# A two-way selective scan: one of four sums moved to TensorE and ScalarE, and decays kept from the forward to the backward pass

## The chip, the cores and the metric

The kernel runs on one core of one Trainium2 chip. The core has five engines that run beside each other, each through its own instructions in order: TensorE (PE in the profile; PEld are its weight loads), VectorE (DVE), ScalarE (ACT), GpSimd (POOL) and SyncE (SP), which here issues the DMA transfers. SBUF is the large on-chip memory, PSUM the small one that TensorE writes. The metric is the device time of one execution in microseconds; lower is better.

## What is computed

Four images of 64 x 64 pixels with 96 channels go through four layers: a selective-scan block, a convolution, attention with a feed-forward network, and a Fourier filter with a feed-forward network. The change concerns the scan of the first layer. Cut to what matters, the reference is:

```python
x_hwwh = jnp.stack([x_hw, x_wh], axis=0)                       # by rows, by columns
xs = jnp.concatenate([x_hwwh, jnp.flip(x_hwwh, axis=3)], axis=0)   # and both backwards
...
def step(h, inp):
    u_t, dt_t, B_t, C_t = inp
    dA = jnp.exp(dt_t[..., None] * A)                          # the decay
    h = dA * h + (dt_t * u_t)[..., None] * B_t[:, None, :]
    y = jnp.sum(h * C_t[:, None, :], axis=-1)
    return (h, y)
_, ys = jax.lax.scan(step, h0, (uT, dT, BT, CT))
...
yy = y[0] + wh_y + inv_y[0] + invwh_y
```

An image has 192 inner channels with 16 states each and 4096 positions. The forward and the backward scan of one orientation have the same decays `dA`, the same `dt * u * B` and the same `C`, so their states `h` can be added before they are multiplied by `C` and summed over the states.

## The kernel before

**Phases.** A phase is one group of 8 channels (with 16 states: 128 partitions) of one image in one orientation. There are 4 images x 2 orientations x 24 groups = 192 phases (`phases`, N = 192), in a loop over `n` in which the order of every engine's instructions is written out by hand (`manual_schedule`). The 4096 positions are cut into 4 chunks of 1024 (`CH`), numbered q = 0 to 3.

A phase has eight steps. In the first four (a loop over q, with the forward scan at L1677) DVE scans the chunks forwards into `S`, one after the other, each starting from the last column of the one before. In the other four (a loop over k, where k = 0 works on chunk 3 and k = 3 on chunk 0; the scan is at L1722) it scans them backwards. A backward scan writes over its own decays; a copy of one column (`edge`, L1728) carries the state on; then DVE adds the result to the forward one (L1729: `S = S + pa`).

Around DVE's scans:

- `load_delta` and `load_du` (their DMAs are recorded at L1412) fetch delta (`dl`) and delta times u (`B`) by chunk, in the order of SP's queue. `dl` and `S` have five buffers each: `place_of` gives a phase's chunks the places 0 to 3, and the next one's the places 4 to 1, so that a chunk's place comes free for the next phase's chunk 4 - q, and place 0 or 4 for chunk 0 of the phase after that. `B` has eight, two sets.
- `decay` (L1450) on ScalarE makes exp(A x delta) from `dl` into a PSUM buffer `pa`, of which there are two of two banks each. Those of chunks 3 and 2 serve both directions (chunk 2's is made a second time at q = 3, the two at hand then being chunk 3's and this one); those of chunks 1 and 0 are made anew at k = 1 and k = 2, and that of the next phase's chunk 0 at k = 3. That makes seven decays per phase.
- `times_b` (L1440) on POOL multiplies `B` by the states' B, `times_c` (L1444) multiplies the sum `S` by C. Their order in a phase is: at q = 0 to 3 `times_c` of chunk 0 of the phase before, `times_b` of chunk 3, `times_b` of chunks 0 and 1 of the next phase; at k = 0 `times_b` of its chunk 2; at k = 1 to 3 `times_c` of chunks 3, 2 and 1.
- `reduce` (L1460) on TensorE sums over the 16 states, four matmuls for each half of a phase; `result` (L1468) on ScalarE copies that out of PSUM, and `store_result` (L1477) stores it.

**The other stages.** While the scans run, the steps before them for images 1 to 3 (`main_lane`, then `before_scans`: projection, 3 x 3 convolution, gates) and the layers after them for images 0 to 2 (`rest`) are dealt out between the scans by `pieces(step)`: after each of the eight steps a table `gains` gives each engine some credit (the five columns are TensorE, ScalarE, POOL, DVE and DMA issue), and a piece of another stage is placed when its engine's credit covers its cost. They have three PSUM banks; the scans have five (four for the two `pa`, one for `py`). What is left of `rest` when the scans end is put before the last image's own layers.

**The steps that the prediction names:**

```python
later = decay(n, q + 1) if q < 3 else decay(n, 2)          # forward, one chunk ahead
...
nc.vector.tensor_tensor_scan(
    pa[:, ::-1], pa[:, ::-1], Bs[n, q][:, ::-1],
    edge if k else 0.0, ALU.mult, ALU.add,
)
if k < 3:
    edge = big.tile([128, 1], F32, tag="edge", name="edge", bufs=2)
    nc.vector.tensor_copy(edge, pa[:, 0:1])
nc.vector.tensor_tensor(Ss[n, q], Ss[n, q], pa, ALU.add)
```

Of the kernel before, what the change touches and what calls it, by code (L numbers as in the profile page):

```python
# [73 lines left out]
def layers(ctx: ExitStack, tc: tile.TileContext, a: dict, out):  # L74
# [1268 lines left out]
    def main_lane(take):  # L1343

        region = Region(tc)
        wk = region.sbuf("pre")
        images = [before_scans(b, wk, take, prev=b - 1 if b > 1 else None) for b in range(1, NB)]
        yield [chain(*parts) for parts in zip(*images)], [region, weights]
        for b in range(NB - 1):
            yield from rest(b, take, 1)  # L1350
# [17 lines left out]
    def last_place(name, k):  # L1368

        if (name, k) not in last_tiles:  # L1370
            tags = {
                "w_in": [f"B{4 * (N % 2) + q}" for q in range(4)],
                "sz_in": [f"dl{place_of(N - 1, q)}" for q in (3, 2, 1, 0)],
                "xr": [f"rep0{q}" for q in range(4)],
                "y_in": [f"B{4 - 4 * (N % 2) + q}" for q in range(4)],
            }
            t = big.tile([128, CH], F32, tag=tags[name][k // 2], name=name)
            for j in range(2):
                last_tiles[name, k // 2 * 2 + j] = t[:C, j * BLK : (j + 1) * BLK]
        return last_tiles[name, k]  # L1380
# [19 lines left out]
    def place_of(n, q):  # L1400


        return (4, 3, 2, 1)[q] if n % 2 else q
# [41 lines left out]

    def decay(n, q):
        if n < N:
            pa = ps.tile([128, CH], F32, tag="pa", name="pa", bufs=2)
            g = phases[n][1]
            nc.scalar.activation(pa, dls[n, q], AF.Exp, scale=nega[:, g : g + 1])  # L1450
            return pa

    def reduce(n, half):

        if n < 0:
            return
        py = pys[n, half] = ps.tile([128, BLK], F32, tag="py", name="py")
        for j in range(4):
            q, k = 2 * half + j // 2, j % 2
            nc.tensor.matmul(  # L1460
                py[32 * j : 32 * j + 32, :], lhsT=red, rhs=Ss[n, q][:, k * BLK : (k + 1) * BLK],
                start=True, stop=True,
            )

    def result(n, half):
# [17 lines left out]
    class Lane:  # L1483
# [34 lines left out]
    gains = [  # L1518
        (2.6, 0.7, 0, 0.8, 1.8), (1.4, 1.2, 0, 0.8, 0.8),
        (2.6, 1.2, 0, 0.8, 0.8), (2.6, 1.2, 0, 0.8, 0.8),  # L1520
        (3.8, 2.8, 1.2, 1, 1.6), (3.8, 2.4, 1.2, 1, 1.4),
        (3.8, 2.4, 1.2, 1, 1.0), (2.6, 2.4, 1.2, 1, 1.6),
    ]
    cap = (4.4, 3.0, 3.2, 1.6, 4.0)

    def pieces(step):
# [3 lines left out]
        for free, bank in returned:  # L1530
            free.append(bank)
        returned.clear()
        for e in range(5):

            more = 1.25 if e in (2, 4) and clock[0] > 8 * (N - NG) else 1
            credit[e] = min(cap[e], credit[e] + gains[step][e] * more)
        for lane in list(lanes):
# [79 lines left out]
    def first_loads():  # L1617
# [8 lines left out]
        for q in range(NCH):  # L1626
            load_rep(0, 1, q)
        for q in range(3):
            load_du(1, q)
# [16 lines left out]
    with tc.manual_schedule():  # L1646
        ordered[0] = True
        pa = decay(0, 0)
        for n in range(N + 1):
# [3 lines left out]
            for q in range(NCH):  # L1653

                if q == 1:
                    load_du(n + 1, 3)
                if q > 1:
                    load_delta(n + 1, q - 2)
                if n % NG == 0 and 0 < n < N and q > 0:
                    load_rep(h, 1, 4 - q)  # L1660
                later = decay(n, q + 1) if q < 3 else decay(n, 2)
                if q == 0:
                    times_c(n - 1, 0)
                elif q == 1:
                    times_b(n, 3)
                else:
                    times_b(n + 1, q - 2)
                if q == 1:
                    reduce(n - 1, 0)
                if q == 2:  # L1670
                    store_result(n - 1, 1)
                if end:
# [4 lines left out]
                nc.vector.tensor_tensor_scan(  # L1677
                    s, pa, Bs[n, q], Ss[n, q - 1][:, CH - 1 : CH] if q else 0.0, ALU.mult, ALU.add
                )
                if q < 3:  # L1680
                    pa = later
                pieces(q)
# [17 lines left out]
            for k, q in enumerate(reversed(range(NCH))):  # L1700
# [6 lines left out]
                if k == 1:  # L1707
                    store_result(n - 1, 0)
                if k == 2:
                    load_delta(n + 1, 3)  # L1710
                if k > 0:
                    load_du(n + 2, k - 1)
                if n % NG == NG - 2:
                    load_rep(h + 1, 0, k)
                if k == 1:
                    pa, later = later, decay(n, 1)
                elif k == 2:
                    pa, later = later, decay(n, 0)
                elif k == 3:
                    pa, later = later, decay(n + 1, 0)  # L1720

                nc.vector.tensor_tensor_scan(  # L1722
                    pa[:, ::-1], pa[:, ::-1], Bs[n, q][:, ::-1],
                    edge if k else 0.0, ALU.mult, ALU.add,
                )
                if k < 3:
                    edge = big.tile([128, 1], F32, tag="edge", name="edge", bufs=2)
                    nc.vector.tensor_copy(edge, pa[:, 0:1])  # L1728
                nc.vector.tensor_tensor(Ss[n, q], Ss[n, q], pa, ALU.add)  # L1729
                if k == 3:  # L1730
                    reduce(n, 1)
                pieces(4 + k)
                if n == N - 1:
                    for i in (2 * k, 2 * k + 1):
                        last_loads(last_place, i)
            pa = later
            if n % NG == NG - 4 and h + 1 < len(halves):
# [120 lines left out]
```

## Time and profile before

| what | us |
|---|---|
| median of 3 runs (lowest to highest) | 5898.77 (5889.44 to 5907.25) |
| the profiled execution | 5897.32 |
| its span, first to last instruction | 5895.5 |
| first scan starts | 359.2 |
| last sum of the scans ends | 5487.4 |

The mean TensorE clock that was granted in the profiled execution is 0.73 of full speed. The page's second part shows how evenly the middle is filled (40 slices of 147 us, each digit a busy share in tenths):

```profile
PE   8978888889873675553566764656467655566787
...
DVE  2049898899899998999899999999998999989464
ACT  4557766776664356545555456454634554545333
POOL 1258888889898667767678778776866777766300
PEclk9978888889875765566657865676576655785788
DMA  3258878887698878788988868686986568896203
```

To read it: DVE is near nine tenths from slice 4 to slice 37, which are the scans. The last three slices are the last image's layers, where TensorE works most. The DMA row is the mean busy share of the 16 DMA engines.

A row of the costliest groups reads: line, engine and operation, output <- inputs, shape, count | busy us in all, mean ns of one | idle time of the engine just before them, and what ended it. A row of waits reads: who <- for whom: us in all, times, longest.

### The profile page before, as it was taken

The page shows a single profiled execution, that of the slowest core. Times are in us where ns is not written, and L with a number is a line of the kernel's source. Part 1 is how long each engine was busy: PE and PEld are TensorE (multiplying, and loading weights), DVE is VectorE, ACT ScalarE, POOL GpSimd, SP SyncE. Part 2 cuts the span into 40 slices and gives each one's busy share as a digit, 9 for nine tenths or more (in the row PEclk, how much of TensorE's full clock was granted, in tenths as well). Part 3 has the DMA queues.
Part 4 walks back from the last instruction along what each step waited for, and adds up shares of the span by engine and source line. Part 5 has one row for each costly group of instructions (what it writes and reads, how often), then busy time and mean ns, then how long its engine had stood idle before and what let it go on. Part 6 is the DMA issues. An engine that isn't in the chain of part 4 may idle for free. (4 is left out here: it accounts for less than half of the span.)

```text
span 5895.5 us, 64395 instructions
## 1 busy us (share of the span) xinstructions
PE 4072.8 (69%) x19490; PEld 1646.2 (28%) x19490; DVE 4947.4 (84%) x3590; ACT 3235.1 (55%) x4358; POOL 4104.8 (70%) x1982
## 2 busy tenths in 40 slices
PE   8978888889873675553566764656467655566787
PEld 3322222223220121142321211433122114332245
DVE  2049898899899998999899999999998999989464
ACT  4557766776664356545555456454634554545333
POOL 1258888889898667767678778776866777766300
PEclk9978888889875765566657865676576655785788
DMA  3258878887698878788988868686986568896203
GB/s 99 77 158 236 226 208 223 244 243 206 187 248 238 229 199 222 202 227 246 254 228 229 211 169 222 203 239 187 239 224 182 158 190 234 248 242 184 57 30 112
DMA packets 469416, 1173.08 MB, mean 199 GB/s; under 512 B 90496, under 2 KB 155628, under 8 KB 468972
## 3 DMA queue, kind: packets, MB, share of 16 engines
q1 hardware_dynamic: 469068, 1168.97, 71.7%
q8 instruction: 154, 2.52, 0.2%
q14 instruction: 194, 1.59, 0.1%
HBM read 1011.86 MB, written 156.76 MB: 198 GB/s over the span
## 5 line engine op out<-in xcount | busy, mean ns | idle before, releaser
L1444 POOL TENSOR_TENSOR S<-S,rep 128x1024 f32<-128x1024 f32 x768 | 1807.1, 2353 | 965.1 <-DVE S L1729 885.1
L1450 ACT ACTIVATE pa<-dl,nega 128x1024 f32<-128x1024 f32 x1344 | 1498.5, 1116 | 1539.1 <-DVE S L1729 1175.0
L1440 POOL TENSOR_TENSOR B<-B,rep 128x1024 f32<-128x1024 f32 x768 | 1790.8, 2359 | 90.5 <-DMA B<-du_s 45.3
L1677 DVE TENSOR_TENSOR_SCAN S<-pa,S,B 128x1024 f32<-128x1024 f32 x576 | 1352.1, 2347 | 257.3 <-ACT pa L1450 86.1
L1722 DVE TENSOR_TENSOR_SCAN pa<-pa,edge,B 128x1024 f32<-128x1024 f32 x576 | 1354.0, 2351 | 66.7 <-ACT pa L1450 66.6
L1460 PE MATMUL py<-S,red 128*32 128x512 f32 x3072 | 630.9, 886 | 858.9 <-POOL S L1444 785.1
L361 PE MATMUL p_conv<-xp,conv_w 96*96 96x504 f32 (+3 forms) x2304 | 1056.4, 613 | 13.6 <-ACT u L374 11.5
L1729 DVE TENSOR_TENSOR S<-S,pa 128x1024 f32<-128x1024 f32 x768 | 932.2, 1214 | 6.6
L1677 DVE TENSOR_TENSOR_SCAN S<-pa,B 128x1024 f32<-128x1024 f32 x192 | 438.0, 2281 | 176.7 <-DMA rep<-bc_s 173.1
L361 PEld LDWEIGHTS p_conv<-xp,conv_w 96*96 96x96 f32 x2304 | 386.1, 171 | 669.0 <-issue 615.5
L1722 DVE TENSOR_TENSOR_SCAN pa<-pa,B 128x1024 f32<-128x1024 f32 x192 | 440.8, 2296 | 5.3
L1460 PEld LDWEIGHTS py<-S,red 128*32 128x32 f32 x3072 | 76.0, 128 | 1228.0 <-POOL S L1444 1009.6
L154 ACT COPY side<-side 96x256 f32<-96x256 f32 (+1 forms) x448 | 281.3, 628 | 52.9 <-DMA duT_s<-side 25.9
L1055 POOL CAST h<-y 128x1536 fp8e5<-128x1536 f16 x64 | 95.5, 1493 | 294.7 <-ACT y L766 284.2
L877 PE MATMUL p_mean<-t,centre 96*96 96x512 f32 x256 | 199.5, 895 | 117.7 <-ACT sq L869 48.8
L527 PE MATMUL p_y<-side,ident 96*96 96x512 f32 x336 | 215.2, 792 | 29.9 <-DMA side<-y_s 15.6
L1468 ACT COPY ys<-py 128x512 f32<-128x512 f32 x384 | 221.2, 576 | 19.6 <-PE py L1460 17.3
L929 PE MATMUL p_rstd<-rs_y,pick 32*96 32x512 f32 x256 | 168.4, 985 | 71.0 <-DVE ln L920 23.6
L833 PE MATMUL p_l<-x,taps 96*96 96x504 f32 (+3 forms) x432 | 202.8, 623 | 9.6 <-DMA x<-x 9.6
L1120 PE MATMUL p_h<-w1s,ln 97*64 97x64 f32 x2304 | 177.9, 346 | 36.7 <-DVE hb L1104 18.6
L1046 PE MATMUL p_f<-q,w_L 96*128 96x512 fp8e5 x192 | 98.2, 548 | 149.7 <-ACT y L757 75.6
L1120 PEld LDWEIGHTS p_h<-w1s,ln 97*64 97x64 f32 x2304 | 171.6, 251 | 78.2 <-issue 31.4
(210 smaller groups left out, 5059.4 us busy)
## 6 DMA issues: line engine op xcount, KB each, us to landing
dl<-delta_s SPq DMA_DIRECT2D x768, 256.0 KB
B<-du_s SPq DMA_DIRECT2D x768, 256.0 KB
B<-duT_s SPq DMA_DIRECT2D x768, 256.0 KB
dl<-deltaT_s SPq DMA_DIRECT2D x768, 256.0 KB
z_s<-z SPq DMA_DIRECT2D x48, 512.0 KB
zl<-z_s SPq DMA_DIRECT2D x64, 384.0 KB
side<-y_s SPq DMA_DIRECT2D x120, 192.0 KB
rep<-bc_s SPq DMA_DIRECT2D x64, 256.0 KB
```

What stands on the lines that cost most here:

```text
L154: nc.scalar.copy(o.rearrange("p (w h) -> p w h", h=HW), t[:n, :].rearrange("p (h w) -> p w h", w=HW)[:, q * w : (q + 1) * w, :],)
L361: nc.tensor.matmul(pr[:, ra:rb, ca_:cb_], lhsT=conv_w[:, kc, ky * 3 + kx, oc * C : (oc + 1) * C], rhs=xp[:, kc, at + ra : at + rb, ca_ + d ...
L527: nc.tensor.matmul(p, lhsT=ident[:C, :C], rhs=x, start=(j == 0), stop=(j == 2))
L1120: nc.tensor.matmul(p[at : at + N1, j, :], lhsT=ln3[:, 8 * k + j, :], rhs=w1s[:, hs], start=True, stop=True,)
L1440: nc.gpsimd.tensor_tensor(Bs[n, q], Bs[n, q], reps[n // NG, 0, q], ALU.mult)
L1444: nc.gpsimd.tensor_tensor(Ss[n, q], Ss[n, q], reps[n // NG, 1, q], ALU.mult)
L1450: nc.scalar.activation(pa, dls[n, q], AF.Exp, scale=nega[:, g : g + 1])
L1460: nc.tensor.matmul(py[32 * j : 32 * j + 32, :], lhsT=red, rhs=Ss[n, q][:, k * BLK : (k + 1) * BLK], start=True, stop=True,)
L1468: nc.scalar.copy(ys, pys.pop((n, half)))
L1677: nc.vector.tensor_tensor_scan(s, pa, Bs[n, q], Ss[n, q - 1][:, CH - 1 : CH] if q else 0.0, ALU.mult, ALU.add)
L1722: nc.vector.tensor_tensor_scan(pa[:, ::-1], pa[:, ::-1], Bs[n, q][:, ::-1], edge if k else 0.0, ALU.mult, ALU.add,)
L1729: nc.vector.tensor_tensor(Ss[n, q], Ss[n, q], pa, ALU.add)
```

## The change

Four things are changed together.

1. **One sum of four, on other engines.** From the phase on in which the steps before the scans are done for all images (`done["pre"]`), the sum of k = 3 (chunk 0) is not made by DVE. Instead `add_up` at q = 0 of the next phase lets TensorE add `S` and the backward result, each by two matmuls of 512 columns with the identity matrix, in a PSUM buffer; `take_sum` at q = 1 copies that to `S` on ScalarE. By the order of instructions these are 138 of the 192 phases: 54 to 191.
2. **Decays are kept.** Five decays per phase instead of seven. The two PSUM buffers have names now: chunk 0 and chunk 2 use `pa0`, chunk 3 uses `pa1`; chunk 1's decay is written over `dl` in SBUF and stays there until its backward scan; chunk 0's is made a second time at k = 2, also over `dl`. The backward scan of chunk 1 (k = 2) reads `dl` and writes a PSUM buffer, that of chunk 0 (k = 3) reads `dl` and writes it in place, or writes to PSUM where DVE still adds.
3. **Order.** `times_c` of chunk 0 moves from q = 0 to q = 2, and `times_b` of chunk 3 and of the next chunk 0 come one step earlier; `reduce` of the first half is made in two parts, at q = 1 and q = 3; the loads of du come one step later (chunk 2's at the next q = 0), and that of delta of chunk 3 at k = 3.
4. **Credits.** The table `gains` is changed in four rows, and a second one, `short_gains`, is used from the first moved sum on.

```diff
-    def decay(n, q):
+    def in_psum(first):
+        return ps.tile([128, CH], F32, tag="pa0" if first else "pa1", name="pa")
+
+    def decay(n, q, pa=None):
         if n < N:
-            pa = ps.tile([128, CH], F32, tag="pa", name="pa", bufs=2)
             g = phases[n][1]
+            pa = dls[n, q] if pa is None else pa
             nc.scalar.activation(pa, dls[n, q], AF.Exp, scale=nega[:, g : g + 1])
             return pa
...
+    def add_up(n):
+        if n in added:
+            p = sums[n] = in_psum(False)
+            for k in range(2):
+                half = slice(k * BLK, (k + 1) * BLK)
+                for x, start in ((Ss[n, 0], True), (dls[n, 0], False)):
+                    nc.tensor.matmul(
+                        p[:, half], lhsT=ident, rhs=x[:, half], start=start, stop=not start
+                    )
+
+    def take_sum(n):
+        if n in added:
+            nc.scalar.copy(Ss[n, 0], sums.pop(n))
...
     gains = [
-        (2.6, 0.7, 0, 0.8, 1.8), (1.4, 1.2, 0, 0.8, 0.8),
-        (2.6, 1.2, 0, 0.8, 0.8), (2.6, 1.2, 0, 0.8, 0.8),
-        (3.8, 2.8, 1.2, 1, 1.6), (3.8, 2.4, 1.2, 1, 1.4),
+        (2.6, 0.7, 0, 0.8, 1.8), (2.0, 1.2, 0, 0.8, 0.8),
+        (2.6, 1.2, 0, 0.8, 0.8), (2.0, 2.0, 0, 0.8, 0.8),
+        (3.8, 3.0, 1.2, 1, 1.6), (3.8, 3.0, 1.2, 1, 1.4),
         (3.8, 2.4, 1.2, 1, 1.0), (2.6, 2.4, 1.2, 1, 1.6),
     ]
+    short_gains = [
+        (1.6, 0.7, 0, 0.8, 1.8), (2.2, 0.6, 0, 0.8, 0.8),
+        (2.6, 1.2, 0, 0.8, 0.8), (2.2, 2.0, 0, 0.8, 0.8),
+        (3.8, 3.0, 1.3, 1, 1.6), (3.8, 3.0, 1.3, 1, 1.4),
+        (3.8, 2.6, 1.3, 1, 1.2), (2.6, 1.6, 0.8, 0.8, 1.4),
+    ]
...
+                if q == 0:
+                    load_du(n + 1, 2)
                 if q == 1:
                     load_du(n + 1, 3)
...
-                later = decay(n, q + 1) if q < 3 else decay(n, 2)
                 if q == 0:
+                    pas[1] = decay(n, 1)
+                    times_b(n, 3)
+                    add_up(n - 1)
+                elif q == 1:
+                    if not end:
+                        pas[2] = decay(n, 2, in_psum(True))
+                    times_b(n + 1, 0)
+                    take_sum(n - 1)
+                    reduce(n - 1, 0, (1,))
+                elif q == 2:
+                    if not end:
+                        pas[3] = decay(n, 3, in_psum(False))
                     times_c(n - 1, 0)
-                elif q == 1:
-                    times_b(n, 3)
+                    store_result(n - 1, 1)
                 else:
-                    times_b(n + 1, q - 2)
-                if q == 1:
-                    reduce(n - 1, 0)
-                if q == 2:
-                    store_result(n - 1, 1)
+                    times_b(n + 1, 1)
+                    reduce(n - 1, 0, (0,))
...
-                if k == 2:
+                if 0 < k < 3:
+                    load_du(n + 2, k - 1)
+                if k == 3:
                     load_delta(n + 1, 3)
-                if k > 0:
-                    load_du(n + 2, k - 1)
...
-                if k == 1:
-                    pa, later = later, decay(n, 1)
-                elif k == 2:
-                    pa, later = later, decay(n, 0)
-                elif k == 3:
-                    pa, later = later, decay(n + 1, 0)
+                if k == 2:
+                    pas[0] = decay(n, 0)
+                if k == 3 and n + 1 < N:
+                    first = decay(n + 1, 0, in_psum(True))
+                on_pe = k == 3 and "pre" in done
+                pa = in_psum(False) if k > 1 and not on_pe else pas[q]
                 nc.vector.tensor_tensor_scan(
-                    pa[:, ::-1], pa[:, ::-1], Bs[n, q][:, ::-1],
+                    pa[:, ::-1], pas[q][:, ::-1], Bs[n, q][:, ::-1],
                     edge if k else 0.0, ALU.mult, ALU.add,
                 )
...
-                nc.vector.tensor_tensor(Ss[n, q], Ss[n, q], pa, ALU.add)
+                if on_pe:
+                    added.add(n)
+                else:
+                    nc.vector.tensor_tensor(Ss[n, q], Ss[n, q], pa, ALU.add)
```

## The prediction

> **What bounds the kernel now.** I read the page's busy shares first, then the engines' busy time cut into stages, then the costliest groups, then who waits for whom, and last the order of time at the end of the scans.
>
> The page's first part:
>
> ```profile
> PE 4072.8 (69%) x19490; PEld 1646.2 (28%) x19490; DVE 4947.4 (84%) x3590; ACT 3235.1 (55%) x4358; POOL 4104.8 (70%) x1982
> ```
>
> Busy time by stage. The cuts are mine: the first scan starts at 359, phase 54 at 1794 (138 phases carry the new sum in the changed kernel, so phases 54 to 191), and the last scan ends at 5486.
>
> ```profile
> core 0: us, PE busy (x) PEld busy (x) DVE busy (x) ACT busy (x) POOL busy (x), PEclk, DMA share, GB/s
> 359.00:1794.00 1435.00, 1194.53 (x3064) 383.06 (x3064) 1268.43 (x811) 997.70 (x1341) 1238.88 (x625) 0.84 0.80 224
> 1794.00:5486.00 3692.00, 2220.51 (x12405) 947.42 (x12405) 3455.05 (x2400) 1916.58 (x2540) 2737.49 (x1257) 0.65 0.79 215
> 5486.00:5895.00 409.00, 336.63 (x3276) 195.25 (x3275) 189.64 (x278) 122.80 (x210) 48.22 (x37) 0.85 0.18 59
> ```
>
> In the scans DVE is 88% busy early and 94% late, POOL 86% and 74%. A phase takes 1435/54 = 26.6 us early and 3692/138 = 26.8 us late. What it is made of:
>
> ```profile
> L1444 POOL TENSOR_TENSOR S<-S,rep 128x1024 f32<-128x1024 f32 x768 | 1807.1, 2353 | 965.1 <-DVE S L1729 885.1
> L1450 ACT ACTIVATE pa<-dl,nega 128x1024 f32<-128x1024 f32 x1344 | 1498.5, 1116 | 1539.1 <-DVE S L1729 1175.0
> L1440 POOL TENSOR_TENSOR B<-B,rep 128x1024 f32<-128x1024 f32 x768 | 1790.8, 2359 | 90.5 <-DMA B<-du_s 45.3
> L1677 DVE TENSOR_TENSOR_SCAN S<-pa,S,B 128x1024 f32<-128x1024 f32 x576 | 1352.1, 2347 | 257.3 <-ACT pa L1450 86.1
> L1722 DVE TENSOR_TENSOR_SCAN pa<-pa,edge,B 128x1024 f32<-128x1024 f32 x576 | 1354.0, 2351 | 66.7 <-ACT pa L1450 66.6
> ...
> L1729 DVE TENSOR_TENSOR S<-S,pa 128x1024 f32<-128x1024 f32 x768 | 932.2, 1214 | 6.6
> ```
>
> Call the forward steps q0 to q3, the backward ones k0 to k3 (k0 works on chunk 3). In the order of time a forward scan follows the last after 2.52 us, a backward step with edge copy and sum takes 3.6, and q0 starts 1.14 after k3's sum starts: 24.4 us, which is the distance between q0 starts in 44 of 191 phases. The rest of a phase is DVE work of other stages and waits. Who DVE waits for after 1794:
>
> ```profile
> DVE S L1677 <- ACT pa L1450: 48.8, 32, 4.7
> DVE S L1677 <- DVE S L1677: 23.1, 91, 0.3
> DVE pa L1722 <- ACT pa L1450: 23.0, 12, 7.8
> ```
>
> With 39.8 and 43.6 us before 1794, decays that come late cost 155 us in all. DVE is the bound, but POOL stands close behind it.
>
> The lines that decide my forecast are few. At the end of the scans (view in order of time, DVE, then POOL) operations with both inputs in SBUF meet on the two engines:
>
> ```profile
> 5498.09 3.34 DVE L620 TENSOR_TENSOR y_in<-y_in,sz_in 96x512 f32<-96x512 f32 x2
> 5501.35 0.68 DVE L619 TENSOR_TENSOR y_in<-y_in,w_in 96x512 f32<-96x512 f32 x1
> 5502.06 3.31 DVE L620 TENSOR_TENSOR y_in<-y_in,sz_in 96x512 f32<-96x512 f32 x2
> ```
>
> ```profile
> 5497.95 1.26 POOL L619 TENSOR_TENSOR y_in<-y_in,w_in 96x512 f32<-96x512 f32 x1 [6.77 <-DMA y_in<-y_s]
> 5499.40 1.48 POOL L619 TENSOR_TENSOR y_in<-y_in,w_in 96x512 f32<-96x512 f32 x1 [0.19 <-DMA y_in<-y_s]
> 5501.73 3.10 POOL L619 TENSOR_TENSOR y_in<-y_in,w_in 96x512 f32<-96x512 f32 x2 [0.84 <-DMA y_in<-y_s]
> ```
>
> The same 0.68 us multiply takes 1.67 where POOL is at work: it waits out POOL's operation, and POOL's grow from 1.26 to 1.5. With one input in PSUM nothing of the kind is seen:
>
> ```profile
> L502 DVE TENSOR_TENSOR side<-p_y,side x56: 657/679/689, 1856.0 to 5338.7; 96x512 f32<-96x512 f32 x56
> ```
>
> (minimum, median, maximum in ns; 50 of these 56 ran beside a POOL operation). Every scan and sum of the kernel before has one input in PSUM.
>
> [...]That a scan behaves as a TENSOR_TENSOR does is shown by no scan here, since none reads two SBUF tensors.
>
> **The change, part by part**, against the profiled execution: span 5895.5, time 5897.3, 1.5 below the median of 5898.8.
>
> 1. *k3's sum leaves DVE in 138 phases*: 138 x 1.14 = -157 us. TensorE makes it with 4 matmuls of 512 columns against the identity. No row has 128x128x512; the nearest are p_y against the identity (96x96, 792 ns, L527) and p_mean (895): 2.6 us at least (p_y's with their overlap, 215.2/336 = 0.64 each), 3.6 at most. TensorE is 60% busy late (2220/3692) at clock 0.65; this takes it to 70 to 74%. ScalarE's copy: ys (512 elements) takes 0.576,[...] taken beside DVE's q1. Behind it on ScalarE stands decay q3, on TensorE both halves of `reduce`, on POOL `times_c` of chunk 0 (moved from q0 to q2, behind two `times_b`). If TensorE comes late, q3's decay does too: 0 to 80 us; 40 in the first rival below.
>
> 2. *Two of seven decays per phase go*: 384 x 1.116 = 429 us of ScalarE, which is no bound. What counts is that k0 to k2 wait for no decay and q1's needs no PSUM buffer: of the 155 us I take 70% away, -108; none and all are the ends.
>
> 3. *Where the kept decays lie.* q1's and chunk 0's second decay overwrite delta in SBUF, and B is in SBUF too. So q1, k2 and k3 now read two SBUF tensors: 3 of 8 scans, in all 192 phases. From below this costs nothing[...]; from above, full exclusion. I take exclusion.
>  A late phase, q0 at 0, with POOL operations of 2.33 in their new order: c1 to 2.2; b3 starts at once, to 4.55; q1, ready at 2.5, waits until 4.45 and ends at 6.75; b0, c0, b1, b2 follow it to 15.95; q2, q3, k0, k1 are free of POOL and end with k1's sum at 19.1; c3 is done at 18.3, so k2 goes at once, to 21.5; c2 waits for it and ends at 23.7; k3, ready at 22.75, waits to 23.6 and ends at 25.95. A bare phase is then 25.95 instead of 24.4, although the sum is gone (23.3 without exclusion). [...]other stages' POOL work (19.84 - 18.86 = 1.0 a phase) falls on it mostly, 0.7, and of the 1.9 of their DVE work 1.1 (the rest lies in the waits at q1 and k3): 27.8, against 26.75. 138 x 1.05 = +145; this contains items 1 and 2.
>  An early phase keeps its sum, and POOL has 1238.9/54 = 22.9 us of work in it. With three scans of 2.2 that is 29.5, less some 1.0[...], plus 1.1 of idle where both engines wait for a sum: 29.6, against 26.6. 54 x 3.0 = +163.
>
> 4. *Loads.* delta of q3 is now fetched at k3 (after k2's scan has read delta in place), du of chunk 2 at the next q0. The shortest distance seen from the end of such an issue to its decay is 4.1 us; from k2's end to q3's decay there are some 9. SP is late by 5 us and more in about 30 phases whose DMA engines are over 85% busy (1760 to 1910, 5070 to 5300): nothing while phases are longer, 0 to 90 us otherwise, 60 in the rival.
>
> 5. *The credits.* By the order of instructions, 19 more p_f1 and 18 more p_f2 matmuls of image 2's last feed-forward are left after the last scan, with 28 ScalarE, 35 DVE and 12 POOL operations. At the end of the trace 8 such blocks take 36 us (5856 to 5892); 6 more, half of it beside the last sums: +14 (0 to 27).
>
> Sum: 145 + 163 + 14 = +322, hence 5897 + 322 = 6219, say 6220.
>
> **The rivals.** *A, the scans don't exclude POOL, so it is faster*: -157 - 108 + 40 + 60 + 14 = -151: 5746. For it: no scan with two SBUF inputs is seen; against: the multiply is. It turns where the three scans' waits exceed 151/192 = 0.8 us a phase; I expect 3 to 4.
> *B, exclusion, but waits that mostly fall where DVE waits anyway*: late phases as long as before (26.75), early ones +2: 5897 + 108 + 14 = 6019. For it: the bare late phase leaves 0.8 us[...].
> *C, TensorE at its throttled clock is late every phase* and DVE waits at q3 without exclusion: A plus 1 us in 138 phases, 5884, no change.
>
> **How the numbers follow.** Exclusion as computed 0.52, B 0.16, A 0.28, C 0.04. Likeliest: 6220, in its own case 6080 to 6370. The range 5730 to 6370 leaves about a tenth out on each side. About 0.3% is what tells a change from none: slower 0.68, same 0.03, faster 0.29.
>
> **What would show it.** Right: scans at q1, k2, k3 with means of 3 us and more and others at 2.35; POOL's multiplies longer than 2.36 in the mean; early phases near 29.6, late near 27.8. Wrong: all scans at 2.35, phases near 25.5. If DVE's idle time before q3 grows on ScalarE, items 1 and 4 were too cheap.

## The result, and the profile after

| | us |
|---|---|
| median before (4 runs, 5889.44 to 5907.25) | 5901.62 |
| median after (4 runs, 6669.51 to 6698.51) | 6685.39 |
| ratio, 95% interval | 1.133 (1.1294 to 1.1366) |
| profiled execution after: span | 6694.6 |

The kernel became 13.3% slower: 784 us, where 322 were forecast. The sign and the kind of cause were forecast, the size wasn't, and the time lies above the forecast's 5730 to 6370.

The page's first part, after (PE, DVE, ACT, POOL: busy us, share, instructions):

```profile
PE 4722.5 (71%) x20594; PEld 1868.3 (28%) x20594; DVE 5723.2 (85%) x3479; ACT 2950.2 (44%) x4086; POOL 5150.2 (77%) x1981
```

DVE executes 111 instructions fewer than before and is busy 776 us longer; POOL has one instruction fewer and is busy 1045 us longer. Neither got more to do: in these traces a scan that is kept waiting by POOL counts as busy time too, as one of 12.24 us below shows, where those that read PSUM take 2.35. The same three stages as before, cut at the first scan, at phase 54 and at the end of the last scan:

```profile
core 0: us, PE busy (x) PEld busy (x) DVE busy (x) ACT busy (x) POOL busy (x), PEclk, DMA share, GB/s
357.70:2169.80 1812.10, 1302.90 (x3056) 398.92 (x3056) 1736.94 (x810) 889.70 (x1234) 1547.39 (x626) 0.78 0.63 177
2169.80:6235.90 4066.10, 2721.86 (x13455) 1141.88 (x13456) 3741.40 (x2256) 1719.42 (x2342) 3457.41 (x1244) 0.75 0.71 195
6235.90:6694.60 458.70, 378.94 (x3338) 206.90 (x3337) 210.72 (x312) 142.74 (x242) 64.87 (x48) 0.82 0.17 56
```

An early phase (0 to 53) grew from 26.6 to 1812.1/54 = 33.6 us, a late one (54 to 191) from 26.8 to 4066.1/138 = 29.5, the tail from 409 to 459. That is 54 x 7.0 + 138 x 2.7 + 50 = 800 us. The costliest groups say where:

```profile
L1445 POOL TENSOR_TENSOR S<-S,rep 128x1024 f32<-128x1024 f32 x768 | 2404.8, 3137 | 815.1 <-DVE S L1777 637.9
L1441 POOL TENSOR_TENSOR B<-B,rep 128x1024 f32<-128x1024 f32 x768 | 2090.7, 2741 | 31.5 <-DMA B<-du_s 27.2
...
L1722 DVE TENSOR_TENSOR_SCAN S<-dl,S,B 128x1024 f32<-128x1024 f32 x192 | 1147.2, 5975 | 89.9 <-ACT dl L1456 16.9
...
L1722 DVE TENSOR_TENSOR_SCAN S<-pa,S,B 128x1024 f32<-128x1024 f32 x384 | 901.1, 2347 | 192.7 <-ACT pa L1456 124.5
...
L1767 DVE TENSOR_TENSOR_SCAN pa<-dl,edge,B 128x1024 f32<-128x1024 f32 x246 | 707.8, 2877 | 5.6 <-issue 0.4
...
L1767 DVE TENSOR_TENSOR_SCAN dl<-dl,edge,B 128x1024 f32<-128x1024 f32 x138 | 424.3, 3075 | 3.7 <-ACT dl L1456 3.6
L1482 PE MATMUL pa<-S,ident 128*128 128x512 f32 x552 | 382.1, 782 | 13.9 <-DVE S L1777 13.9
L1482 PE MATMUL pa<-dl,ident 128*128 128x512 f32 x552 | 328.7, 681 | 16.5 <-DVE dl L1767 16.4
L1488 ACT COPY S<-pa 128x1024 f32<-128x1024 f32 x138 | 140.2, 1016 | 241.9 <-PE pa L1482 239.1
```

The form of the operands tells the three disputed scans from the others: those that read `pa` (PSUM) still take 2.35 us, those that read `dl` (SBUF) take 5.98 (q1), 2.88 and 3.08. Above 2.35 each that is 192 x 3.63 + 246 x 0.53 + 138 x 0.73 = some 926 us. POOL's multiplies, 2.35 us before, take 3.14 and 2.74. So the exclusion is there, and q1's mean is the surprise: the forecast had 4.25. In the order of time, DVE and then POOL, around one q1 of the early stage:

```profile
802.05 2.28 DVE L1722 TENSOR_TENSOR_SCAN S<-pa,B 128x1024 f32<-128x1024 f32 x1
804.62 12.24 DVE L1722 TENSOR_TENSOR_SCAN S<-dl,S,B 128x1024 f32<-128x1024 f32 x1 [0.29 <-issue]
817.05 2.35 DVE L1722 TENSOR_TENSOR_SCAN S<-pa,S,B 128x1024 f32<-128x1024 f32 x1 [0.19 <-DMA y_s<-ys]
```

```profile
801.90 2.34 POOL L1445 TENSOR_TENSOR S<-S,rep 128x1024 f32<-128x1024 f32 x1
804.20 1.26 POOL L464 TENSOR_TENSOR u<-r,u 96x512 f32<-96x512 f32 x1
805.43 4.65 POOL L1441 TENSOR_TENSOR B<-B,rep 128x1024 f32<-128x1024 f32 x2
810.04 2.35 POOL L1445 TENSOR_TENSOR S<-S,rep 128x1024 f32<-128x1024 f32 x1
812.35 6.66 POOL L1441 TENSOR_TENSOR B<-B,rep 128x1024 f32<-128x1024 f32 x2
```

The scan is ready at 804.6 and isn't let in at 805.4, 807.7, 810.0 or 812.3, when POOL goes from one operation to the next; it ends at 816.9, so it ran from about 814.6, and then POOL's operation is the one that is held (6.66 us for two). That was the last operation of the row: the scan was let in ahead of it. The forecast let a waiting scan in after one operation.

### The profile page after: what moved, and what is told of

Its sections match the earlier page's. It is cut to its first block, busy times and chain, and to the rows that moved or that the text cites. A ratio compares the mean times of both kernels' runs of the same rounds, so it can differ in the third digit from the quotient of the medians.

```text
span 6694.6 us, 65666 instructions
## 1 busy us (share of the span) xinstructions
PE 4722.5 (71%) x20594; PEld 1868.3 (28%) x20594; DVE 5723.2 (85%) x3479; ACT 2950.2 (44%) x4086; POOL 5150.2 (77%) x1981
## 5 line engine op out<-in xcount | busy, mean ns | idle before, releaser
L1445 POOL TENSOR_TENSOR S<-S,rep 128x1024 f32<-128x1024 f32 x768 | 2404.8, 3137 | 815.1 <-DVE S L1777 637.9
L1722 DVE TENSOR_TENSOR_SCAN S<-dl,S,B 128x1024 f32<-128x1024 f32 x192 | 1147.2, 5975 | 89.9 <-ACT dl L1456 16.9
L1722 DVE TENSOR_TENSOR_SCAN S<-pa,S,B 128x1024 f32<-128x1024 f32 x384 | 901.1, 2347 | 192.7 <-ACT pa L1456 124.5
L1456 ACT ACTIVATE pa<-dl,nega 128x1024 f32<-128x1024 f32 x576 | 641.9, 1116 | 787.5 <-DVE S L1777 445.5
L1767 DVE TENSOR_TENSOR_SCAN pa<-dl,edge,B 128x1024 f32<-128x1024 f32 x246 | 707.8, 2877 | 5.6 <-issue 0.4
L1767 DVE TENSOR_TENSOR_SCAN pa<-pa,edge,B 128x1024 f32<-128x1024 f32 x192 | 451.3, 2351 | 0.0
L1456 ACT ACTIVATE dl<-dl,nega 128x1024 f32<-128x1024 f32 x384 | 439.0, 1143 | 2.4 <-DMA dl<-delta_s 2.2
L1767 DVE TENSOR_TENSOR_SCAN dl<-dl,edge,B 128x1024 f32<-128x1024 f32 x138 | 424.3, 3075 | 3.7 <-ACT dl L1456 3.6
L1482 PE MATMUL pa<-S,ident 128*128 128x512 f32 x552 | 382.1, 782 | 13.9 <-DVE S L1777 13.9
L1482 PE MATMUL pa<-dl,ident 128*128 128x512 f32 x552 | 328.7, 681 | 16.5 <-DVE dl L1767 16.4
```

What stands on the lines that cost most here:

```text
L1445: nc.gpsimd.tensor_tensor(Ss[n, q], Ss[n, q], reps[n // NG, 1, q], ALU.mult)
L1482: nc.tensor.matmul(p[:, half], lhsT=ident, rhs=x[:, half], start=start, stop=not start)
L1722: nc.vector.tensor_tensor_scan(s, pas[q], Bs[n, q], Ss[n, q - 1][:, CH - 1 : CH] if q else 0.0, ALU.mult, ALU.add,)
L1767: nc.vector.tensor_tensor_scan(pa[:, ::-1], pas[q][:, ::-1], Bs[n, q][:, ::-1], edge if k else 0.0, ALU.mult, ALU.add,)
```

## The experiments

A *row* below is a run of POOL operations without a gap between them. Two theories stood at first: that a waiting scan lets POOL's row pass, as the 12.24 us above suggest (W in the expectations), and the forecast's, that it gets in after one operation and the long scans have another cause (A). A third came out of the second kernel: it gets in after one operation, unless the row contains a narrow one, on fewer than 128 partitions (N). Where kernels are compared with before, the runs of before are those taken beside them (medians 5906 to 5911).

**meet: one scan against a row, by itself.** A kernel of its own, which computes nothing of the reference: N multiplies of 128x1024 on POOL, and one scan that is ready while the first of them runs. In short:

```diff
+for i in range(n):
+    nc.gpsimd.tensor_tensor(gs[i % 6], gs[i % 6], rep, ALU.mult)
+nc.vector.tensor_copy(fill[:, :filler], pd[:, :filler])
+nc.vector.tensor_tensor_scan(s, dec, b, 0.0, ALU.mult, ALU.add)
```

> A kernel of its own that computes nothing of the reference: DVE runs one scan of 128x1024 while POOL works through N multiplies of 128x1024 (2.34 us each) that wait for nothing; the scan starts some 0.5 us after the first multiply. Theory W (a scan that reads two SBUF tensors is let in only when POOL's row of ready instructions comes to its end, just ahead of the last of them): the scan's duration grows with N, about 4 us for N = 1 and 2, then 2.3 us more for each further multiply, 13 us for N = 6. Theory A (the prediction's: one operation of POOL is waited for, then the scan is let in): about 4 us for every N. Both: 2.35 us with the decay in PSUM. With POOL's third multiply waiting for ScalarE, W says about 4 us, since the ready row is then two long. Half-size multiplies, 12 of them: W 13 us, A 3 us. A multiply on DVE with both inputs in SBUF instead of the scan: W 12 us, A 3 us.

The view in order of time, DVE, with rows of one and of six, and with six and a scan that reads PSUM:

```profile
16.54 4.27 DVE L1818 TENSOR_TENSOR_SCAN s<-dec,b 128x1024 f32<-128x1024 f32 x1
...
64.07 4.17 DVE L1818 TENSOR_TENSOR_SCAN s<-dec,b 128x1024 f32<-128x1024 f32 x1
...
80.38 2.28 DVE L1818 TENSOR_TENSOR_SCAN s<-pd,b 128x1024 f32<-128x1024 f32 x1
```

About 4.2 us whatever the length of the row: the rest of one operation and the scan's own 2.3. The whole-row theory falls for such rows, and the forecast's one operation holds. The rows also show, with nothing else beside them, what the forecast could show for a multiply alone (1.67 against 0.68 us): a scan with two SBUF inputs is held up, 4.17 us against 2.28 with one in PSUM. A DVE multiply of 128x1024 with two SBUF inputs, in the place of the scan, took 3.10; the kernel's sums of that shape, with one input in PSUM, take 1.21.

**meet2: what is different in the kernel.** The same with one thing changed in each row: start value from SBUF, a later start, tiles that a DMA or ScalarE wrote, and a row that opens with a 96x512 multiply, as L464 is.

> A second kernel of its own that computes nothing of the reference. The first one showed one operation waited for however long POOL's row was, so theory W as stated is not enough; here the same row of N multiplies meets the scan in forms nearer to the kernel: with the scan started late (it must wait for DVE's operation just before it), with a start value read from SBUF, right behind another scan whose last column is its start value (as q1 behind q0), and with the tiles of POOL's multiplies freshly loaded by DMA or written by ScalarE, so that each multiply carries a wait already over. If a late start of the scan is what lets POOL's row go first: about 4, 8, 13 us for N = 2, 4, 6 in the first four, and the same behind another scan. If the start value in SBUF does it: 13 us for N = 6 with an old value too. If POOL's waits do it: 13 us only with the loads or ScalarE's writes. If none of it, all are at 4.2 us or below and the cause lies elsewhere. With the decay in PSUM 2.35 us.

All took 4.25 us or less except the last: 15.25, the whole row. (The same row without its narrow multiply: 2.53.)

**hold: give POOL a reason to stop at q1.** If rows are the trouble, a break in them mends it. After with a POOL copy that waits for q1's scan, and `times_b` behind it.

```diff
-                    times_b(n + 1, 0)
+                    if end:
+                        times_b(n + 1, 0)
...
+                if q == 1:
+                    nc.gpsimd.tensor_copy(seen, s[:, :1])
+                    times_b(n + 1, 0)
```

> The changed kernel with POOL made to wait for the scan of q1 ahead of its multiply for B of chunk 0 (a copy of one column of that scan's result stands before it), so that POOL's ready row ends at q1. W: q1's scan falls from a mean of 5.98 us to about 3.2, early phases from 33.6 to about 29.4 us, late ones from 29.5 to about 28.5 (the 14 or so late rows that cost 10 us and more go): about 6340 us. A: the row's length does not matter, POOL only gets another wait: 6690 us or more.

6442.55 us, 1.0908 (1.0888 to 1.0927) of before, between the two forecasts. q1 fell and k2 rose:

```profile
L1772 DVE TENSOR_TENSOR_SCAN pa<-dl,edge,B 128x1024 f32<-128x1024 f32 x246 | 956.4, 3888 | 6.6 <-DMA rep<-bcT_s 1.3 <-issue 0.5
L1724 DVE TENSOR_TENSOR_SCAN S<-dl,S,B 128x1024 f32<-128x1024 f32 x192 | 632.6, 3295 | 88.6 <-ACT dl L1456 22.8 <-PE py L1468 10.7 <-issue 10.7
```

q1 went from 5.98 to 3.30 us, but k2's early scans from 2.62 to 5.62: the narrow operations now stand in the row ahead of k2. Of the scans with two SBUF inputs that had to wait, 72 in the kernel after had an operation on fewer than 128 partitions earlier in their row; 65 of these were passed over at the first change of operation, and the mean of the 72 is 10.0 us. Of the other 289, 284 were let in at the first change; their mean is 3.46. In hold 65 of 73 were passed over with a narrow operation and 5 of 268 without. (What counts as a wait or as one row moves these counts by ten or so, hold's 5 by up to 17.) That is an association; the next kernels test it as a cause.

**meet3 and meet4: which operation does it.** Rows of six 128x1024 multiplies behind one other operation, and variants.

```diff
+elif x:
+    p, w = x
+    nc.gpsimd.tensor_tensor(other[:p, :w], other[:p, :w], rep[:p, :w], ALU.mult)
```

> A third kernel of its own that computes nothing of the reference. In the second one only one row made the scan wait to its end (15.25 us): the row that opened with a multiply of 96x512. Here a row of POOL's multiplies of 128x1024 holds one other multiply, and the scan (both inputs in SBUF) comes right behind a scan from PSUM. Theory N[...]: after 96x512, 96x1024, 64x512 and 32x512 at the head the scan takes 13 to 16 us, with two or four multiplies behind it 5 and 9 to 11; after 128x512 and 128x64 at most 4. Rival L (an operation of another length does it, by 512 or 64 columns): 13 to 16 us after 128x512 and 128x64 as well, and not after 96x1024. With 96x512 in third place and the scan asked for ahead of it, both 2.5 us; in second place and asked for behind it, N 10 us or more; with 128x512 there, N at most 4. With POOL made to wait for ScalarE behind the 96x512, N at most 4.5: the wait mends it. From PSUM 2.35 us.

> A fourth kernel of its own that computes nothing of the reference, for what the third left open: whether it is the partitions alone, for how long it lasts, and what happens when the scan asks during the narrow multiply. Theory N: with 96x1024 at the head and the scan asked for one operation later, the scan waits out the row, about 14 us; with 128x1024 in its place at most 2.6. The scan asked for within the 96x512 itself: 16 to 17 us as most q1 scans of the changed kernel, or 3.0 as four of them. Two narrow ones at the head as one: 16 to 17 us from wherever the scan asks. The state lasts: with the scan asked for three and four operations behind a 96x512 some 10.5 and 8 us. If the state passed with time or with the next operation, these two would be below 4.5; if 96x1024 does nothing, it is the mix of lengths and partitions, not the partitions.

The view of meet3 in order of time, all engines:

```profile
16.31 1.26 POOL L1832 TENSOR_TENSOR other<-other,rep 96x512 f32<-96x512 f32 x1
17.53 13.82 POOL L1836 TENSOR_TENSOR g<-g,rep 128x1024 f32<-128x1024 f32 x6
18.25 15.24 DVE L1817 TENSOR_TENSOR_SCAN s<-dec,s,b 128x1024 f32<-128x1024 f32 x1
...
34.13 1.26 POOL L1832 TENSOR_TENSOR other<-other,rep 128x512 f32<-128x512 f32 x1
35.35 15.80 POOL L1836 TENSOR_TENSOR g<-g,rep 128x1024 f32<-128x1024 f32 x6
36.16 3.67 DVE L1817 TENSOR_TENSOR_SCAN s<-dec,s,b 128x1024 f32<-128x1024 f32 x1
```

Both opening operations take 1.26 us. Behind that on 96 partitions six multiplies pass in 13.82 us and the scan comes last; behind that on 128 the scan is let in behind the first of the six, and the six take 15.80. What the rest gave ("six" are multiplies of 128x1024):

| row ahead of the scan | scan, us |
|---|---|
| 96x512, 64x512 or 32x512, then six | 15.2 |
| 96x512, then two / four | 5.97 / 10.56 |
| 96x512, then six, asked for during the third / fourth of them | 10.50 / 8.18 |
| 96x512, then six, asked for during the 96x512 itself | 16.75 |
| 128x1024, then 96x512 (or 128x512), then five, asked for behind the second | 12.83 (3.64) |
| two or three of 128x1024, then 96x512, asked for ahead of it | 2.45, 2.40 |
| two of 96x512, or 96x512 and 32x512, then six | 16.5 |
| 128x512 or 128x64, then six; 128x1024, then six, asked for one operation later | 3.67, 2.73; 2.42 |
| **96x1024**, then six (meet3; asked for one operation later in meet4) | 2.51; 2.57 |
| 96x512, then a POOL operation that waits for ScalarE, then six | 4.51 |
| 96x512, then six, scan reads PSUM | 2.35 |

The third theory missed with 96x1024: in these rows it isn't narrowness alone (2.51 us), but an operation that is narrow and also shorter than those behind it (15.24). Whether it must be shorter than they are, or short by itself, no row tells apart. Here the scan is kept out until the row ends or POOL waits (4.51). The kernel isn't so simple. There some two thirds of the scans that were passed over got in between two operations (as at 814.6 above), some of them right behind a second 96x512; and four q1 scans that asked during a 96x512 took 2.97 to 2.99 us, not meet4's 16.75. What makes this state, and what else ends it, no run shows.

**wide: take the narrow operations out of the kernel.** After, with POOL's softplus and du multiplies and its feed-forward sum made on 128 partitions instead of 96 (the added rows hold padding), at the same places.

```diff
-                    p, give = yield from take("p_dt")
+                    R = 128 if b else C
+                    p, give = yield from take("p_dt", R)
...
-                    add_engine.tensor_tensor(t[:, blk(i)], t[:, blk(i)], z, ALU.add)
+                    W = 128 if ordered[0] else C
+                    add_engine.tensor_tensor(wide_t[:W, blk(i)], wide_t[:W, blk(i)], wide_z[:W], ALU.add)
```

> The changed kernel with the multiplies and sums of other stages on POOL (softplus and du, the feed-forward's sum) widened from 96 to 128 partitions, with rows that nobody reads; POOL's time for them stays 1.26 us each, ScalarE fills a few rows (below 60 us in all). N: no narrow operation stands in POOL's rows, so a scan waits for one operation: q1's mean falls from 9.6 to about 3.3 us early and from 4.6 to about 3.6 late, phases to about 29 and 28.5 us: 6310 us (6220 to 6420). L: nothing changes, 6690 us.

6417.83 us, 1.0854 (1.083 to 1.0877): 268 us of the 784 come back, though POOL's operations only became wider. It is inside the forecast's range, at its upper end. The group of q1, by form:

```profile
L1748 DVE TENSOR_TENSOR_SCAN S<-dl,S,B 128x1024 f32<-128x1024 f32 x192 | 684.5, 3565 | 121.5 <-ACT dl L1482 35.9 <-PE py L1494 32.7 <-POOL S L1471 9.2
```

q1 takes 3.57 us, k2 and k3 about 3.0; 371 of the 384 scans that waited were let in at the first change of operation, and an early phase is 30.4 us. So the narrow operations are a cause in the kernel too. They aren't the only one: eleven backward scans of wide's early phases took 6.8 to 10.1 us though their rows, a mix of 128x512 and 128x1024, held nothing narrow. In the order of time, DVE and then POOL:

```profile
706.53 9.54 DVE L1793 TENSOR_TENSOR_SCAN pa<-dl,edge,B 128x1024 f32<-128x1024 f32 x1
```

```profile
705.54 1.28 POOL L477 TENSOR_TENSOR w<-w,e 128x512 f32<-128x512 f32 x1
706.79 2.35 POOL L1471 TENSOR_TENSOR S<-S,rep 128x1024 f32<-128x1024 f32 x1
709.09 1.27 POOL L479 TENSOR_TENSOR r<-r,lg 128x512 f32<-128x512 f32 x1
710.33 2.34 POOL L1471 TENSOR_TENSOR S<-S,rep 128x1024 f32<-128x1024 f32 x1
712.63 1.27 POOL L481 TENSOR_TENSOR r<-r,w 128x512 f32<-128x512 f32 x1
```

This scan, too, runs only when the row has ended, at 713.9; why, no run shows. Wide and hold are both some 8 to 9% slower than before: in wide 516 of the 784 us remain, though nearly all of its waiting scans (371 of 384) are let in at the first change of operation.

**psum, psum_g, q1psum, nosum: the parts one by one.** nosum is after without the sum on TensorE; q1psum is nosum with chunk 1's decay in PSUM, made again at k1; psum is nosum with every decay in PSUM (six a phase), so that no scan reads two SBUF tensors; psum_g is psum with the credits of before.

```diff
-                on_pe = k == 3 and "pre" in done
+                on_pe = False
...
-                    pas[1] = decay(n, 1)
+                    pas[1] = decay(n, 1, in_psum(False)) if not end else None
...
+                if k == 1:
+                    pas[1] = decay(n, 1)
```

(The first lines are nosum's, the others q1psum's.)

> The changed kernel with all sums on DVE, its credits and order kept; the decays stay in SBUF. W: POOL's multiply of chunk 0 no longer waits for ScalarE's copy of the sum, so the rows in the late phases grow as long as in the early ones and q1 waits there too: q1's mean 9 to 12 us in all phases, late period about 33.5 us, 7250 us in all. A: only the sum's 1.14 us come back, 138 x 1.14 = 157 at the most and by the gaps in the trace about half: 6770 to 6850 us.

> The changed kernel with all sums on DVE and all decays in PSUM (six of them per phase: chunk 2's is still kept from q2 to k1), its credits, order of POOL's multiplies and loads kept. W and A: no scan reads two SBUF tensors, all take 2.35 us, and the phases are those of the kernel before or a little shorter: 5830 us (5780 to 5920). Rival C (the new order, loads or credits cost the time, not the place of the decays): over 6100 us.

> Run nosum (all sums on DVE) with the decay of q1 in PSUM and that of chunk 1 made again, at k1, in place of delta: k2 and k3 read two SBUF tensors, q1 no longer does. If the waits at q1 are the price (9.1 us early, 4.1 late in nosum), early phases fall from 33.2 to about 29 us and late ones from 29.4 to 27.7, and some of POOL's rows meet k2 and k3 instead: 6210 us (6120 to 6350), that is two thirds of the way from nosum to psum. If each of the three scans costs the same, a third of the way: 6440.

> Run psum with the credits of the kernel before. If the new credits lengthened the tail (451 us in psum against 409 before), the tail falls back to about 410 and the whole to 5920 us. If the tail comes from elsewhere, 5960.

| kernel | median us | ratio (95%) | early / late phase, us | q1 / k2 / k3 early, us |
|---|---|---|---|---|
| after | 6685.39 | 1.133 (1.1294 to 1.1366) | 33.56 / 29.46 | 9.57 / 2.62 / 3.51 |
| nosum | 6674.76 | 1.132 (1.1283 to 1.1357) | 33.23 / 29.44 | 9.12 / 2.66 / 3.48 |
| q1psum | 6213.19 | 1.0516 (1.0498 to 1.0534) | 28.98 / 27.77 | 2.35 / 3.37 / 4.15 |
| psum | 5962.26 | 1.0093 (1.0073 to 1.0114) | 27.11 / 26.65 | 2.35 / 2.35 / 2.35 |
| psum_g | 5921.65 | 1.0022 (1.0013 to 1.0031) | 26.97 / 26.83 | 2.35 / 2.35 / 2.35 |

Down this table q1's decay in SBUF costs 462 us, k2's and k3's together 251, the credits 41, and 13 to 20 are left against before. The sum on TensorE makes no difference that stands out of the noise (11 us; the intervals of after and nosum overlap). Both forecasts for nosum, 7250 and 6770 to 6850, missed: the rows at q1 didn't grow in the late phases, and no time was lost without the moved sum. psum lies 42 us above its range, about what the credits cost. Most scans of psum, on the page:

```profile
L1723 DVE TENSOR_TENSOR_SCAN S<-pa,S,B 128x1024 f32<-128x1024 f32 x576 | 1352.1, 2347 | 292.1 <-ACT pa L1456 116.2
...
L1770 DVE TENSOR_TENSOR_SCAN pa<-pa,edge,B 128x1024 f32<-128x1024 f32 x576 | 1353.8, 2350 | 72.0 <-ACT pa L1456 71.7
```

They have the durations of the kernel before to a thousandth. It is the place of the decays that costs, and hardly the new order, which psum_g has too.

**wide_nosum: the sum with the rows mended.** wide with `on_pe = False`.

> Run nosum (all sums on DVE) with the same widening. N: q1 falls as in run wide: about 6330 us. What it tells of the sum on TensorE: if its 1.14 us a phase were lost only in POOL's long rows, run wide is 100 to 150 us faster than this one[...].

6395.25 us, 1.0819 (1.0785 to 1.0853), 23 us below wide and within the intervals of both: here too the moved sum brings nothing. Where its gain goes can be read by step. Mean times of the late phases in the traces, us: q0 runs from its start to q1's, q1 is the scan alone, q2 and q3 each run from the end of the scan ahead to their own end, and the rest follows up to the next q0:

| | q0 | q1 | q2 | q3 | k0, k1 and sums | k2 | k2's sum | k3 | k3's sum | phase |
|---|---|---|---|---|---|---|---|---|---|---|
| nosum | 2.75 | 4.12 | 2.71 | 2.94 | 8.00 | 2.69 | 1.66 | 3.18 | 1.38 | 29.44 |
| after | 2.92 | 4.60 | 3.07 | 3.33 | 8.05 | 2.74 | 1.50 | 3.07 | 0.15 | 29.43 |

1.23 us are saved behind k3, and 0.17 + 0.48 + 0.36 + 0.39 = 1.40 lost from q0 to q3: 0.48 of it as a longer wait for POOL inside q1's scan, the rest as idle time of DVE. Who DVE waits for after phase 54, in the kernel after and then in nosum:

```profile
DVE S L1722 <- ACT pa L1456: 108.6, 58, 7.2
DVE ln L920 <- PE p_rstd L929: 30.5, 13, 5.7
```

```profile
DVE S L1722 <- ACT pa L1456: 40.1, 20, 7.2
```

q3's decay needs the PSUM buffer in which the sum was made. So it stands behind DVE's last scan, TensorE's four matmuls and ScalarE's copy (1.02 us), and the waits of the forward scans for decays in PSUM rose from 40.1 us (20 waits) to 108.6 (58). That is 0.5 us a phase, about half of it ahead of q3; why q1's scan and q2's decay wait longer too isn't shown. In the busy sums TensorE's four matmuls, which stand in the trace as eight records (1104 in 138 phases), take 710.8/138 = 5.15 us a phase, with TensorE 67% busy late at a clock of 0.75.

**six, shared, shared2: can the parts pay in another way?** six is before with chunk 2's decay kept in PSUM from q2 to k1 (six decays). shared is six with the sum of chunk 0 on TensorE by halves through the bank of `py`, so that no decay's buffer is taken; k3's scan still reads its decay from PSUM. shared2 has its last steps later.

```diff
+    def add_half(n, k):
+        if n in added:
+            p = sums[n, k] = ps.tile([128, BLK], F32, tag="py", name="p_sum")
...
+    def take_half(n, k):
+        if n in added:
+            nc.scalar.copy(Ss[n, 0][:, k * BLK : (k + 1) * BLK], sums.pop((n, k)))
...
-            ys = yss[n, half] = big.tile([128, BLK], F32, tag="ys", name="ys", bufs=2)
+            ys = yss[n, half] = big.tile([128, BLK], F32, tag="ys", name="ys", bufs=1)
```

> The kernel before with one edit: the decay of chunk 2 made for q2 is kept for k1 (as the changed kernel does), so six decays a phase, all in PSUM, and the order, the loads, the sums and the credits of before. By the prediction's item 2 a third to a half of what keeping decays can bring, as far as decays come late at all: 5870 us (5840 to 5910). Rival: k1's decay never came late, so nothing: 5905.

> A kernel that takes the sum of the change and leaves its decays: run six (six decays, all in PSUM, order and credits of before), where from the same phase on k3's scan reads PSUM and writes into delta's place, TensorE adds chunk 0 in two halves of 512 columns through the PSUM bank of the results, ScalarE copies each, POOL's multiply of chunk 0 comes at q3 and its reduction at k0; S gets a sixth place. No scan reads two SBUF tensors. If DVE bounds a late phase there, 138 x 1.14 = 157 us go: 5745 us, and some 1.0 of them net: 5770 (5740 to 5850). If TensorE and ScalarE are late with the halves, DVE waits at q3 and k1 and nothing is gained or it loses: 5900 or more.

> Run shared with its steps for the sum set later, so that no engine stands waiting for them: ScalarE's second half and POOL's multiply of chunk 0 at k0, the reduction at k1, the copy of the results behind the decay at k2. If run shared lost because decays stood behind waiting copies on ScalarE (116 and 86 us of DVE's waits there) and TensorE's other matmuls behind the reduction, most of the 157 us now comes: 5800 to 5860 us. If the sum takes too much of TensorE itself (70% busy at a clock of 0.76), other stages stay late and it remains at 5950 us or more.

six: 5900.15 us, 0.9987 (0.998 to 0.9994) of before, the only kernel ahead of it, by a tenth of a per cent, and close to its rival's 5905. shared: 6010.09, 1.0176 (1.0157 to 1.0194); shared2: 6127.51, 1.037 (1.0339 to 1.0401). Both miss the gain that was hoped for, and the later steps made it worse. All their scans take 2.35 or less. From the late waits of shared2 (DVE, TensorE, ScalarE):

```profile
DVE S L1720 <- ACT pa L1452: 341.0, 112, 17.0
...
PE p_sum L1474 <- ACT ys L1483: 448.4, 94, 20.1
...
ACT ys L1483 <- DMA yT_s<-ys: 202.2, 40, 11.0
ACT ys L1483 <- DMA y_s<-ys: 183.2, 43, 18.7
```

With one buffer left for `ys`, ScalarE waits for the store, and what stands behind it in ScalarE's order, decays too, waits with it; TensorE waits for the bank of `py`, in which the results and the sum now take turns. The one `ys` buffer alone is at most a small part of the price: the early phases of both have it too, without the moved sum, and take 26.71 us (shared) and 26.37 (shared2) against 26.38 in six, while the late ones take 27.51 and 28.50 against 26.81. How much the buffer, the bank or TensorE's own time adds there isn't shown. Whether a moved sum can pay where it takes no buffer and no bank that the loop turns over stays open: that wasn't tried.

## Why the prediction was right and wrong

The forecast for the profiled execution was 6219; it took 6696.5, 477 us more. They are about 54 x (33.56 - 29.6) = 214 early, 138 x (29.46 - 27.8) = 229 late and 35 in the tail.

**Item 3, right in kind, the failed step.** That the three scans exclude POOL and that the change is slower for it was right (psum, whose scans take 2.35 us or less in the mean, is 723 us faster than after; rivals A and B fall, and C's late TensorE is real but small beside this). What failed is "waits until 4.45": a scan gets in after one POOL operation. That is so for rows of full-width multiplies (4.17 us), and I had drawn the phase from these alone. The other stages' POOL work was added as an amount, 1.0 us a phase late, though its form matters more: a 96x512 operation in the row can keep the scan out for several operations (12.24 us in the kernel) or to the row's end (15.24 in meet3). Early, where the softplus and du operations (L456 to L464) of the steps before the scans are placed, q1 took 9.57 us against the 4.25 of the hand-made schedule. Taking the narrow operations away, in wide, gives back 54 x 3.19 = 172 of the 214 us early and 138 x 0.77 = 106 of the 229 late, more than half of the error; the phase without them, 30.4 us early in wide, was forecast at 29.6.

**The late phase.** Its three scans, 4.57 + 2.73 + 3.07 = 10.4 us, are close to the 9.85 of the forecast, and the 0.7 us that it set aside for other POOL work covers the difference. That is partly luck: most late scans wait for less than was drawn (the three sum to 9.3 us in wide), and a few rows with a narrow operation make up for it. Two other terms were too small. "The rest lies in the waits": I let 0.8 us of other stages' DVE work a phase vanish in the waits at q1 and k3. In the trace DVE's instructions follow one another, and none of them stands within the 12.24 us of the scan above: the wait hides nothing of its own. The late phase has about 1.9 us of such work, outside the scans. And the bare phase had no late decays, where 129 us, 0.9 a phase, were waited. 25.95 + 0.5 + 1.9 + 0.9 = 29.3, against 29.46: the sum closes, but no run changed these two terms by themselves.

**Item 1, wrong.** The 1.14 us a phase left DVE as computed, ScalarE's copy took 1.02, and the saving came to nothing: -157 was followed by at least the same amount at q0 to q3. I had put the price of the chain at 0 to 80 us and overlooked that it also holds one of two decay buffers; the waits for decays that rose with it are some 70 us, the rest of the loss is not explained. TensorE's time was half of what it should have been: "2.6 us at least, 3.6 at most" took one record of the trace for one matmul, but these f32 matmuls stand as two each (p_y has 336 records for 56 blocks of three), so the same prices give 5.1 to 7.2 us, and 5.15 was measured.

**Item 2, half right.** Early, waits for decays fell from 83 to 18 us, 79%, where 70% was forecast. Whether the fewer decays did it or the longer phases is open: in wide, which keeps the same decays in early phases 3.2 us shorter, with a little more work on ScalarE, they are 82 again. Late, they rose from 72 to 129 with the sum and fell to 58 without. Keeping decays is worth little where it was tried by itself: six has one fewer and gains 0.13%.

**Item 4, right.** Two loads moved, delta's of chunk 3 and du's of chunk 2; the other loads of du stayed in their steps. DVE's waits for loads of delta are 1.5 us early and 5.0 late. **Item 5, mis-sized**: the tail grew by 50 us, not by 14; psum_g, with the old credits, has a tail of 404 us against psum's 452, so the credits made it.

## What to carry to other kernels

Before an operand is moved from PSUM to SBUF, count the SBUF inputs of the DVE instruction that reads it, and look at what GpSimd runs beside it: with a second SBUF input, DVE's scan waited for GpSimd's operation (4.17 us against 2.28 in meet), and where the row contained a 96x512 operation, often for several more (12.24 in the kernel) or for all of it (15.24 in meet3). Work moved off the engine that bounds a loop brought nothing in the forms tried here, each with a chain that came back late and took a buffer or a bank that the loop turns over. In a hand-made schedule, work of the waiting engine itself is not to be counted as hidden in its wait: DVE has no other instruction in the 12.24 us of that scan.

## What the hardware showed that was not expected

- In most rows a waiting scan got in after one POOL operation (4.2 us for rows of one to six), but one 96x512 multiply at the head of six of 128x1024 kept it out to the end (15.24), while 128x512 (3.67), 128x64 (2.73) and 96x1024 (2.51) didn't. In the kernel wide some rows that mix 128x512 and 128x1024 did so too (9.54).
- What keeps the scan out outlasted the 96x512 operation: a scan that asked four operations later still took 8.18 us. Behind a POOL operation that had waited for ScalarE a scan took 4.51.
- The same six multiplies took 13.82 us in a row that let no scan in, and 15.80 with the scan between: 1.98 more for POOL, where such a scan takes 2.28 from PSUM. POOL's multiplies in the kernel rose from 2.35 to 3.14 and 2.74 us.
